# Attention over kept tokens: a step planner that places work by half steps, with row operands made earlier, norms tied to the scores of their step, and an early token load split in two

## The chip, the cores and the metric

The kernel runs on one core of one Trainium2 chip. The time is the device time of one execution in microseconds (us), the median over runs. Matrix products run on TensorE (PE in the profile, its weight loads PEld), sums and element-wise work on VectorE (DVE), exponentials and most copies out of PSUM on ScalarE (ACT), gathers and scatters of rows by index are issued from GpSimd (POOL), and all other transfers from SyncE (SP).

## The reference

```python
# x: (16, 512, 1024), mask: (16, 1024) of 0 and 1, 8 heads of 64
xt = transpose(x, (0, 2, 1))
q = xt @ Wq.T                                   # queries, keys and values are the same
scores = (1/8) * einsum('bhqd,bhkd->bhqk', qh, qh)
logits = (scores * cmask + (1 - cmask) * -1e30) * rmask
attn = softmax(logits)
ctx = einsum('bhqk,bhkd->bhqd', attn, qh)
out = x + transpose(ctx @ Wo.T, (0, 2, 1))
```

A masked key has no weight, and a masked query row sees all logits equal, so that its result is the mean of all values. About half of the 1024 tokens of a batch are kept.

## The kernel before

For each of the 16 batches, `slots` and `index` compute from the mask where each kept token goes (room for C = 544: four chunks of 128 and a tail of 32), and `gather` fetches the rows of the kept tokens in five transfers (L313). `xt` transposes the five chunks on PE (L398) and splits them into two float16 parts (high on ACT, L358; low on DVE, L359). `query(e, g)` makes a 128-row block e of q over half g of the tokens in 12 float16 matmuls (L421); ACT copies it out of PSUM (L424). `qsplit` splits q again (DVE), and SP spreads the parts over partitions (tiles `xx`, L442 to L445). `value(e)` transposes q back (L467), `value_tail` does so for the 32 tail tokens (L484, read out by DVE in L487). `top` (PE L509, DVE L511) and `bottom` (PE L518) turn row sums of squares into a bound for the exponent (`nm`).

`scores` makes 128 rows of scores of one head in four float16 matmuls (L580; the tails of four heads in L555) into one of two PSUM buffers of the tile `pss`, and ACT takes the exponential with its row sum (L584). So the third block of scores waits for the exponential of the first. `attend` multiplies two heads' weights with the values (eight float32 passes, `pav`, L598), and a fifth part covers the tail (L601). `recip_sums` and `recip_rows` make the reciprocals of the sums: DVE work, a PE transpose (L634), a copy `rr` (L637), a write to DRAM `rd`, and a broadcast read `rb`. `norm` multiplies `c` by `rb` (L665), fills the masked rows with the mean and splits the result into `ch` and `cl`. `project(i)` is 12 matmuls of 512 columns (L681), an addition to the token rows (`plus`, L686), and a scatter (L765). `project_tail` does the tails of up to three batches at once, and `rest` adds a mean row to the masked tokens (L752) and scatters them. `sum_half` (L343, ACT) sums token rows loaded in L337 and L348.

All PE results other than `pss` and `pav` share two PSUM buffers of the tile `pm`: the third user waits until the first has been read out.

The order is planned by hand in `run`. While batch b goes through 18 steps (two heads, 128 rows each; two steps are for tails), the list `m` holds other work with a PE cost in us beside each entry: tokens, queries and values of batch b+1, projections of batch b-1, the index of batch b+2. Each step first does what `free` holds for it, then both scores, then takes entries of `m` up to its even share, then two attends:

```python
ps = [self.scores(b, 2 * p, i)]
if i == 2 and whole:
    whole.pop()()
ps.append(self.scores(b, 2 * p + 1, i))
...
goal = total * (st + 1) / N
while pos < len(m) and (done + m[pos][0] / 2 <= goal or st == N - 1):
```

`late`, `gather` and `scatter` go to two lists, from which one transfer leaves per step; each waits for the latest matmul of scores or queries (`beat`). The additions of `rest` wait for `beat` as well. A scheduler behind the language may still move single instructions against the written order.

Of the kernel before, what the change touches and what calls it, by code (L numbers as in the profile page):

```python
# [49 lines left out]
class Fast:  # L50
# [114 lines left out]

    def slots(self, b0, b1):
# [7 lines left out]
        mb = self.sb([P, B, TB], F32, "sc", 3)  # L174
        nc.vector.tensor_scalar(mb, self.mt[:, bs], 0.5, None, ALU.is_gt)
        mh = self.sb([P, B, TB], F16, "tmp", 2)
        nc.vector.tensor_copy(mh, mb)
# [19 lines left out]
        ge = self.sb([P, NC, NB - 1], F16, "c", 3)  # L197
# [5 lines left out]
        oh = self.sb([P, NC, NB], F16, "c", 3)  # L203
# [6 lines left out]
    def facts(self, b0, b1):  # L210

# [17 lines left out]
        eh = self.sb([P, B], F16, "tmp", 2)  # L229
        nc.vector.tensor_copy(eh, e)  # L230
        pe = self.pm([P, B])
        nc.tensor.matmul(pe, lhsT=self.on16, rhs=eh, start=True, stop=True)
# [3 lines left out]

    def index(self, b):
        nc = self.nc
        s = self.st[b]
        ol = self.sb([P, TB, P], F16, "tmp", 2)  # L240
        lo = self.lo[:, b]
        nc.vector.tensor_tensor(ol, self.io128.unsqueeze(1).broadcast_to([P, TB, P]),
                                lo.unsqueeze(2).broadcast_to([P, TB, P]), ALU.is_equal)
# [185 lines left out]
    def qsplit(self, b, e):  # L429


        nc, s = self.nc, self.st[b]
        q = s["q"][:, e, :C]
        hl = self.sb([P, 3, C], F16, "hl", 2)
        nc.vector.tensor_copy(hl[:, 0, :], q)
        nc.vector.tensor_tensor(hl[:, 1, :], q, hl[:, 0, :], ALU.subtract)
        nc.vector.tensor_copy(hl[:, 2, :], hl[:, 0, :])
        xx = self.sb([P, 4, C], F16, "xx", 5)

        def spread():  # L440
            lo, up = slice(0, DK), slice(DK, P)
            nc.sync.dma_start(out=xx[lo, 0:2, :], in_=hl[lo, 0:2, :])  # L442
            nc.sync.dma_start(out=xx[up, 0:2, :], in_=hl[lo, 1:3, :])
            nc.sync.dma_start(out=xx[lo, 2:4, :], in_=hl[up, 0:2, :])
            nc.sync.dma_start(out=xx[up, 2:4, :], in_=hl[up, 1:3, :])  # L445

        self.later(spread)
        s["xx"].append(xx)
# [23 lines left out]

    def value_tail(self, b, g):
# [6 lines left out]
        q = self.sb([P, 2, HG, CT], F32, "qt")  # L480
        nc.scalar.copy(q, s["q"][:, 2 * g:2 * g + 2, 512:C].unsqueeze(2).broadcast_to([P, 2, HG, CT]))
# [13 lines left out]
    def shift(self, b, g):  # L495
        self.top(b, g)
        self.bottom(b, g)

    def top(self, b, g):

        nc, s = self.nc, self.st[b]
        hs = slice(HG * g, HG * g + HG)
        wide = self.smcol[g]
        sm = wide[:, :HG]
        nc.vector.tensor_reduce(sm.rearrange("p (e h) -> p e h", h=2),
                                s["sd"][:, 2 * g:2 * g + 2, :].rearrange("p e (k h) -> p e h k", h=2), AX.X, ALU.max)
        nc.vector.tensor_tensor(sm, sm, s["sdt"][:, hs], ALU.max)
        pt = self.pm([P, P])
        nc.tensor.transpose(pt, wide, self.ident)  # L509
# [32 lines left out]
    def scores(self, b, p, i):  # L542
# [6 lines left out]
        if i is None:  # L549
# [12 lines left out]
            hi = self.sb([P, C], F32R, "c", 3)  # L562
# [26 lines left out]
    def attend(self, b, p, i, ps):  # L589
# [13 lines left out]
        if i == 4:  # L603
            c = self.sb([P, C], F32, "c", 3)
# [41 lines left out]
    def norm(self, b, p):  # L646
# [18 lines left out]
        nc.vector.tensor_tensor(c, c, s["rb"][p], ALU.mult)  # L665
# [109 lines left out]
    def last(self, b, todo):  # L775
# [8 lines left out]
        self.recip(b, 3)  # L784
# [5 lines left out]
        for i in range(4):  # L790
            self.product(s["ch"], s["cl"], slice(i * P, (i + 1) * P), pos[i], range(3))
        self.norm(b, 3)
# [4 lines left out]
    def run(self, flag):  # L797
# [32 lines left out]
        for c in range(DC):  # L830
            self.load("q", c, 0)
        self.slots(0, 2)
        self.warm(36)
        self.index(0)
# [16 lines left out]
        def index1():  # L851
            with self.behind(self.last_xs):
                self.index(1)

        g1 = [(0, L(self.gather, 1, j)) for j in range(5)]

# [7 lines left out]
        first += [(0, lambda k=k: self.load_half(1, k, self.last_xt)) for k in range(DC)]  # L864
        first += value(0, 1) + [(0, L(self.value_tail, 0, 0))] + query(0, 2, 0) + g1[2:3] + query(0, 2, 1)[:1] + g1[3:4]
# [16 lines left out]
        begin = g1[4:] + [(1.5, lambda: None)] + query(0, 3, 0) + value(0, 2) + query(0, 3, 1) + value(0, 3)  # L882
        begin += [(0.3, L(self.value_tail, 0, 1)), (0, L(self.means, 0))]
# [4 lines left out]
        for b in range(B + 1):  # L888
            o, n = b - 1, b + 1
            if b == B:  # L890
                self.last(o, todo)
                break
            free, early, late = {}, ([], []), []
            if b >= 1:
                early = [(0, L(self.recip_sums, o, 3))], [(0.1, L(self.recip_rows, o, 3))]
                late = [(0, L(self.norm, o, 3))]
            if n < B:
                if b in tails:
                    free[0] = [L(self.late, o, 4)]
                    late += [(2.6, L(self.project_tail, o))]  # L900
                for x in rests.get(b, []):
                    free.setdefault(0, []).extend(L(self.late, x, j) for j in range(5, 9))
                    late += [(0, L(self.rest, x, j)) for j in range(5, 9)]
            chunk2 = [(0, L(self.norm, o, 2))] if b else []
            P_ = (lambda *i: project(o, *i)) if b else (lambda *i: [])
            tp, bt = [(0.1, L(self.top, b, 1))], [(0.1, L(self.bottom, b, 1))]
            if n < B:
                m = xt(n)[:1] + early[0] + xt(n)[1:2] + chunk2 + xt(n)[2:3] + early[1] + xt(n)[3:] + tp + query(n, 0, 0) + query(n, 0, 1) + bt + value(n, 0)
                m += query(n, 1, 0) + late + P_(0) + query(n, 1, 1) + P_(1)
                m += [(0, L(self.range_x, n, c)) for c in range(DC)]  # L910
                r = P_(2) + value(n, 1) + [(0.25, L(self.value_tail, n, 0))] + query(n, 2, 0) + query(n, 2, 1)
                r += query(n, 3, 0) + [(0.1, L(self.top, n, 0))] + value(n, 2) + query(n, 3, 1)
                r += [(0.1, L(self.bottom, n, 0))] + P_(3) + value(n, 3)
                r += [(0.25, L(self.value_tail, n, 1)), (0, L(self.means, n))]
                if b + 2 < B:
                    m += [(0.5, L(self.index, b + 2))]
                    r[1:1] = [(0, L(self.gather, b + 2, j)) for j in range(5)]
                if b == 0:
                    for c in range(DC):
                        r.insert(1 + 3 * c, (0, L(self.split, "o", c)))  # L920
                m += r
            else:

                places = [("xi", 8), ("xa", 13)]
                come = [[L(self.late, x, j, *places[k % 2]) for j in range(5, 9)] for k, x in enumerate(rests[b])]
                leave = [[L(self.rest, x, j) for j in range(5, 9)] for x in rests[b]]
                free[0] = [L(self.late, b, 4)] + come[0]
                for c, l in zip(come[1:] + [[]], leave):
                    free[0] += c + l
                m = chunk2 + early[0] + early[1] + tp + bt + [(2.6, L(self.project_means, b))] + late + P_(0, 1, 2, 3)  # L930
            for g in groups:
                if b == g[0] - 1:
                    m.insert(7, (0.1, L(self.facts, *g)))
                if b == g[0] - 2:
                    m.insert(7 if b == 0 else 0, (0.1, L(self.slots, *g)))
            if b == 1:
                m += [(0, L(self.range_w, "o", c)) for c in range(DC)]
            if b == B - 1:
                m.append((0.1, self.ranges))
            if b == 0:  # L940
                m = begin + m
            if b + 2 < B:
                self.start(b + 2)
                for c in range(DC):
                    at = 3 * c + (0 if b else 4)
                    free.setdefault(at, []).append(L(self.load_all, b + 2, c, None if b else first_top))
                    free.setdefault(at + 4, []).append(L(self.sum_half, b + 2, c))
            if b == 0:
                for k in range(3, 2 * DC):
                    if k >= DC:  # L950
                        free.setdefault(0, []).append(lambda k=k: self.load_half(1, k, first_top))
                    free.setdefault(k // 3, []).append(L(self.sum_half, 1, k))
            total = sum(c for c, _ in m)
            done, pos = 0.0, 0
            for st, (p, i) in enumerate(S):
                soon, self.soon = self.soon, []
                for f in soon + free.get(st, []):
                    f()
                if i is None:
                    self.scores(b, p, None)  # L960
                else:
# [181 lines left out]
```

## Time and profile before

| what | value |
|---|---|
| median of three runs | 1109.42 us (1104.3 to 1111.29) |
| profiled execution | 1102.9 us, of which span 1100.9 us |
| granted TensorE clock, mean | 0.997 |
| PE matmuls | busy 1066.3 us, 97% of the span |
| PE weight loads | 695.1 us |
| DVE | 735.7 us, 67% |
| ACT | 675.8 us, 61% |
| POOL | 295.2 us |

The busy time of PE counts each matmul from its start to its modelled end. Neighbours overlap, so a busy PE can still make pauses. The timeline gives the start of each matmul, and the distance from one start to the next tells the pace.

### The profile page before, as it was taken

How to read it: one execution, taken by the hardware profiler on the slowest of the kernel's cores; microseconds unless marked ns; L12 is line 12 of the kernel's file. 1: busy time of each engine (PE TensorE's matmuls, PEld its weight loads, DVE VectorE, ACT ScalarE, POOL GpSimd, SP SyncE). 2: the span in 40 equal slices, each digit the busy share in tenths (PEclk: the TensorE clock that was granted, in tenths of full speed). 3: DMA queues.
4: the chain of work that ended last, by engine and by line, in shares of the span. 5: the costliest groups of instructions: out<-in, count | busy, mean ns of one | idle time of the engine just before them, and what ended most of it. 6: DMA issues, size and time to landing. Idle time of an engine off the chain costs nothing.

```text
span 1100.9 us, 23215 instructions
## 1 busy us (share of the span) xinstructions
PE 1066.3 (97%) x8386; PEld 695.1 (63%) x8386; DVE 735.7 (67%) x2375; ACT 675.8 (61%) x1716; POOL 295.2 (27%) x303
## 2 busy tenths in 40 slices
PE   6899999999999999999999999999999999999997
PEld 6576666666666666666666666666666666666553
DVE  6797467765765757767674766856667675757653
ACT  5786566666666756657665666666656666655550
POOL 3101031323202222222322223232222322223652
PEclk9999999999999999999999999999999999999999
DMA  6755455646546464665655666455664655555752
GB/s 206 213 159 158 128 166 150 191 132 183 153 130 179 125 196 142 183 185 157 184 142 176 175 183 178 138 175 151 204 176 138 185 147 161 150 156 160 222 163 89
DMA packets 78121, 181.34 MB, mean 165 GB/s; under 512 B 15008, under 2 KB 16800, under 8 KB 78000
## 3 DMA queue, kind: packets, MB, share of 16 engines
q1 hardware_dynamic: 56816, 111.62, 36.3%
q0 software_dynamic: 21184, 68.18, 19.2%
q8 instruction: 68, 1.11, 0.4%
q14 instruction: 53, 0.43, 0.1%
HBM read 92.34 MB, written 33.91 MB: 115 GB/s over the span
## 4 chain that ended last, share of the span: by engine, by line
PE 72%; DVE 14%; DMA 6%; issue 4%; ACT 3%; SPq 1%; POOL 0%; DVEq 0%; POOLq 0%; ACTq 0%
PE pav L598 20%; PE pss L580 17%; PE pm L681 15%; PE pm L421 8%; PE pm L398 3%; PE pav L601 2%; DMA rb<-rd 2%; PE pm L467 2%; DVE c L665 2%; PE pm L634 1%; DMA rd<-rr 1%; ACT p L584 1%; PE pss L555 1%; DVE top L366 1%; DVE tmp L458 1%
## 5 line engine op out<-in xcount | busy, mean ns | idle before, releaser
L584 ACT ACTIVATE p<-pss,nm 128x544 f32<-128x544 f32 x512 | 363.2, 714 | 215.2 <-PE pss L580 208.0
L580 PE MATMUL pss<-xx 128*128 128x272 f16 x2048 | 301.6, 280 | 0.1
L598 PE MATMUL pav<-p,v 128*64 128x272 f32 x2048 | 278.8, 402 | 0.9 <-ACT c L605 0.9
L580 PEld LDWEIGHTS <-xx 128*128 128x128 f16 x2048 | 192.1, 99 | 77.9 <-issue 33.7
L598 PEld LDWEIGHTS pav<-p,v 128*64 128x64 f32 x2048 | 130.3, 136 | 98.4 <-issue 40.1
L421 PE MATMUL pm<-xh,wqh 128*128 128x274 f16 (+1 forms) x512 | 143.4, 280 | 0.1
L765 POOL DMA_INDIRECT y_out<-xa,idx x68 | 69.4, 1021 | 275.2 <-PE pss L580 169.5
L421 PE MATMUL pm<-xl,wqh 128*128 128x274 f16 (+1 forms) x512 | 142.9, 279 | 0.2 <-DVE xl L359 0.2
L421 PE MATMUL pm<-xh,wql 128*128 128x274 f16 (+1 forms) x512 | 143.1, 279 | 0.0
L313 POOL DMA_INDIRECT xa<-x_in,idx x68 | 68.7, 1010 | 183.8 <-PE pss L580 89.4
L421 PEld LDWEIGHTS <-wqh 128*128 128x128 f16 x1024 | 99.4, 99 | 23.1 <-issue 5.1
L584 ACT ACTIVATION_READ_ACCUMULATOR p<-pss,nm 128x1 f32 x512 | 102.8, 201 | 0.0
L313 POOL DMA_INDIRECT xi<-x_in,idx x60 | 61.8, 1030 | 142.7 <-PE pss L555 50.8
L686 DVE SCALAR_TENSOR_TENSOR xa<-pm,xa 128x512 f32<-128x512 f32 x60 | 41.4, 689 | 80.6 <-PE pm L681 80.4
L765 POOL DMA_INDIRECT y_out<-xi,idx x60 | 67.1, 1119 | 99.1 <-PE pss L580 51.0
L424 ACT ACTIVATE q<-pm 128x272 f32<-128x272 f32 (+1 forms) x128 | 51.1, 399 | 65.6 <-PE pm L421 65.1
L681 PE MATMUL pm<-woh,cl 128*128 128x512 f16 x240 | 91.0, 379 | 0.0
L681 PE MATMUL pm<-wol,ch 128*128 128x512 f16 x240 | 90.9, 379 | 0.0
L681 PE MATMUL pm<-woh,ch 128*128 128x512 f16 x240 | 90.9, 379 | 0.0
L665 DVE TENSOR_TENSOR c<-c,rb 128x544 f32<-128x544 f32 x64 | 46.3, 723 | 49.1 <-DMA rb<-rd 42.3
L681 PEld LDWEIGHTS <-ch 128*128 128x128 f16 x480 | 46.1, 98 | 40.4
L343 ACT ACTIVATE xm<-xm 128x1024 f32<-128x1024 f32 (+1 forms) x60 | 61.9, 1032 | 2.3 <-DMA xm<-x_nat_in 2.3
(191 smaller groups left out, 1560.8 us busy)
## 6 DMA issues: line engine op xcount, KB each, us to landing
xx<-hl SPq DMA_DIRECT2D x256, 136.0 KB
xm<-x_nat_in SPq DMA_DIRECT2D x56, 512.0 KB
rb<-rd SPq DMA_DIRECT2D x128, 136.0 KB
pt<-c SPq DMA_DIRECT2D x64, 136.0 KB
pt<-p SPq DMA_DIRECT2D x64, 136.0 KB
ub<-ud SPq DMA_DIRECT2D x16, 256.0 KB
xi<-x_nat_in SPq DMA_DIRECT2D x8, 256.0 KB
xa<-x_in,idx POOLq DMA_INDIRECT x68, 4.3
```

The costliest lines, as they stand in the source:

```text
L313: dma = self.nc.gpsimd.indirect_dma_start(out=tile[:n], out_offset=None, in_=self.x, in_offset=bass.IndirectOffsetOnAxis(ap=idx, axis=0))
L343: self.nc.scalar.activation(s["xm"][k], s["xm"][k], AF.Copy, accum_out=s["ms2"][:, k:k + 1])
L398: self.pe = nc.tensor.transpose(pt[:, c, :], x[:n, c * P:(c + 1) * P], self.ident[:n, :n]).ins
L421: self.beat = nc.tensor.matmul(pq, lhsT=w[:, c, e * P:(e + 1) * P], rhs=xx[:, c, cols], start=(k == 0), stop=(k == 3 * DC - 1)).ins
L424: nc.scalar.activation(s["q"][:, e, cols], pq, AF.Copy, scale=1.0 / (SX * SW))
L580: self.beat = nc.tensor.matmul(pt[:, g, :CH], lhsT=xx[:, 2 * k, i * P:(i + 1) * P], rhs=xx[:, 2 * k + a, g * CH:(g + 1) * CH], start=(a == ...
L584: self.exp = [nc.scalar.activation(t.rearrange("p (g c) -> p g c", g=2), pt[:, :, :CH], AF.Exp, bias=s["nm"][p // HG][:, p % HG:p % HG + 1 ...
L598: nc.tensor.matmul(s["pav"][k * DK:(k + 1) * DK, g, :CH], lhsT=s["v"][p][:, i, k * DK:(k + 1) * DK], rhs=ps[k][:, cols], start=(i == 1), s ...
L665: nc.vector.tensor_tensor(c, c, s["rb"][p], ALU.mult)
L681: nc.tensor.matmul(po[:cols.stop - cols.start], lhsT=a[:, e, cols], rhs=w[:, e, :], start=(e == 0 and k == 0), stop=(e == DC - 1 and k == 2))
L686: self.nc.vector.scalar_tensor_tensor(x, po, 1.0 / (SX * SW), x, ALU.mult, ALU.add)
L765: dma = self.nc.gpsimd.indirect_dma_start(out=self.out, out_offset=bass.IndirectOffsetOnAxis(ap=idx, axis=0), in_=x, in_offset=None)
```

## The change

The planner takes entries of `m` at two places of a step, between the two scores and after the attends, by a share for each (`share`). Some functions are cut in two, so that the DVE or ACT part stands earlier in the order than the matmul which uses it: `active` out of `slots`, `facts_sums` out of `facts`, `hot` out of `index`, `tail_copy` out of `value_tail`, `peaks` out of `top`. The order of `m` is new. `norm` of the first three head pairs waits for `beat`, and the first two come two steps later; the tile `c` has four buffers in place of three. Of batch 1, the second four loads of tokens come right behind the first spread of `xx` instead of after the first bound, all eight sums are placed in the steps of batch 0 (three of them are done twice: 75 sums in place of 72), and its first two `xt` come while batch 0 is being set up. In `last`, the reciprocal rows are transposed after a first part of a projection. The computation is the same: the number of matmuls does not change. The core of the diff:

```diff
-        ol = self.sb([P, TB, P], F16, "tmp", 2)
+    def hot(self, b):
+        ol = self.st[b]["ol"] = self.sb([P, TB, P], F16, "tmp", 2)
...
+    def tail_copy(self, b, g):
+        q = s["qt"] = self.sb([P, 2, HG, CT], F32, "qt")
+        self.nc.scalar.copy(q, s["q"][:, 2 * g:2 * g + 2, 512:C].unsqueeze(2).broadcast_to([P, 2, HG, CT]))
...
+    def peaks(self, b, g):
+        sm = self.smcol[g][:, :HG]
...
         nc.vector.tensor_tensor(sm, sm, s["sdt"][:, hs], ALU.max)
+    def top(self, b, g):
+        pt = self.pm([P, P])
+        nc.tensor.transpose(pt, self.smcol[g], self.ident)
...
-            hi = self.sb([P, C], F32R, "c", 3)
+            hi = self.sb([P, C], F32R, "c", 4)
...
-        nc.vector.tensor_tensor(c, c, s["rb"][p], ALU.mult)
+        self.once(nc.vector.tensor_tensor(c, c, s["rb"][p], ALU.mult), self.beat if p < 3 else None)
...
-        self.recip(b, 3)
+        self.recip_sums(b, 3)
...
             self.product(s["ch"], s["cl"], slice(i * P, (i + 1) * P), pos[i], range(3))
+            if i == 0:
+                self.recip_rows(b, 3)
...
+        def rest1():
+            with self.behind(self.last_xx):
+                for k in range(DC, 2 * DC):
+                    self.load_half(1, k)
...
-                m = xt(n)[:1] + early[0] + xt(n)[1:2] + chunk2 + xt(n)[2:3] + early[1] + xt(n)[3:] + tp + query(n, 0, 0) + query(n, 0, 1) + bt + value(n, 0)
-                m += query(n, 1, 0) + late + P_(0) + query(n, 1, 1) + P_(1)
-                r = P_(2) + value(n, 1) + [(0.25, L(self.value_tail, n, 0))] + query(n, 2, 0) + query(n, 2, 1)
-                r += query(n, 3, 0) + [(0.1, L(self.top, n, 0))] + value(n, 2) + query(n, 3, 1)
-                r += [(0.1, L(self.bottom, n, 0))] + P_(3) + value(n, 3)
-                r += [(0.25, L(self.value_tail, n, 1)), (0, L(self.means, n))]
-                    m += [(0.5, L(self.index, b + 2))]
-                    r[1:1] = [(0, L(self.gather, b + 2, j)) for j in range(5)]
+                    m = sums + pk(b, 1) + x[:2] + second + x[2:4] + rows + x[4:]
+                    m += q(0, 0) + tp(b, 1) + q(0, 1)
+                    m += bt(b, 1) + q(1, 0) + v(0) + third + q(1, 1)
+                    m += tc(0) + rng[:2] + tail + v(1) + P_(0) + tv(0) + rest + P_(1) + hot + rng[2:] + q(2, 0) + index
+                    m += pk(n, 0) + q(2, 1) + tp(n, 0) + P_(2) + take + v(2) + q(3, 0) + bt(n, 0)
+                    m += q(3, 1) + tc(1) + [(0, L(self.means, n))] + P_(3) + v(3) + tv(1)
...
+                share = [(1.2, 0) if i is None else ((0.95, 0.95), (0.9, 0), (0.45, 0.95), (0.9, 0))[i] for _, i in S]
+                unit = sum(c for c, _ in m) / sum(map(sum, share))
...
                         ps = [self.scores(b, 2 * p, i)]
                         if i == 2 and whole:
                             whole.pop()()
+                    fill(share[st][0], st == N - 1)
+                    if i is not None:
+                        ps.append(self.scores(b, 2 * p + 1, i))
...
-                            free.setdefault(st + 5, []).append(L(self.norm, b, p))
+                                free.setdefault(min(st + 7, N - 1), []).append(L(self.norm, b, p))
```

## The prediction

> **What bounds the kernel now.** First the page: span, busy times and clock.
>
> ```profile
> span 1100.9 us, 23215 instructions
> ...
> PE 1066.3 (97%) x8386; PEld 695.1 (63%) x8386; DVE 735.7 (67%) x2375; ACT 675.8 (61%) x1716; POOL 295.2 (27%) x303
> ...
> PEclk9999999999999999999999999999999999999999
> ```
>
> PE is the bound, and its clock is granted throughout, so time can only come out of its pauses. The 97% hides them, because overlapping matmuls are counted to their modelled ends. So, second, the timeline of PE, where the distance between starts is the pace.
>
> ```profile
> 345.46 1.09 PE L580 MATMUL pss<-xx 128*128 128x272 f16 x8
> 346.39 0.27 PE L509 MATMUL pm<-ident,smcol 128*128 128x128 f32 x1
> 346.50 0.60 PE L467 MATMUL pm<-ident,q 128*128 128x128 f32 x4
> 347.77 0.33 PE L634 MATMUL pm<-ident,rcol 128*128 128x128 f32 x1 [0.67 <-DVE m L511]
> 347.94 1.09 PE L580 MATMUL pss<-xx 128*128 128x272 f16 x8
> ```
>
> Eight score matmuls take 0.93 us to the next start, 0.116 each; a transpose takes 0.11. The four of L467 should be over at 346.94, yet L634 starts at 347.77: a pause of 0.83, of which the row's busy account shows 0.67. It waits for PSUM: the third user of `pm` needs the buffer of `top` (L509), which DVE's L511 reads late.
>
> Measured so, one pace per form: scores 2048 x 0.116 = 237.6 us; queries 1536 x 0.116 = 178.2; projections 852 x 0.216 = 184.0; attends 2048 x 0.124 (16 in 1.98 in the chain) = 253.5; their tails 256 x 0.125 = 32.0; tail scores 512 x 0.029 = 14.8; float32 transposes 672 x 0.109 = 73.2; the rest 17. Sum 990. From the first matmul (3.5) to the last (1093.3) are 1090 us, so **about 99 us are pauses**: 18 before 66 us, 77 from 66 to 1056, 3 to 4 behind. Of the 77, about 39 are what each change of kind takes everywhere (0.09 from float16 into an attend, 0.15 from `bottom`, 0.03 between attends), and **38 are waits**. By the matmul that waits: L634 11.5, scores 8.4, `xt` 7.5, `value` 5.0, others 6.
>
> Third, who ends PE's waits (total, times, longest), and the same for DVE.
>
> ```profile
> PE pm L634 <- DVE m L511: 5.5, 8, 0.9
> ...
> PE pss L398 <- DMA xa<-x_in,idx: 3.4, 1, 3.4
> PE pm L398 <- DVE tmp L487: 3.1, 3, 1.3
> PE pss L555 <- DMA xx<-hl: 2.7, 1, 2.7
> PE pm L634 <- DVE rcol L628: 2.4, 4, 0.8
> ```
>
> ```profile
> DVE c L665 <- DMA rb<-rd: 42.3, 27, 4.7
> ...
> DVE xi L752 <- PE pss L580: 17.2, 20, 1.9
> ```
>
> Many short waits for PSUM to be read out, two long ones in the head. DVE's 42.3 us on `rb` are no cost by themselves.
>
> **The change part by part.** For each wait I count, in the instruction order of both programs, the PE work that stands between cause and consumer (cover), priced by the pace.
>
> *1. Reciprocal rows, L634.* Before, 14 times the buffer of `top` is needed again after at most 0.93 us of work (0.44 in nine). After, one or two such places remain. The wait for the sums themselves (L628, L625: 3.0 of the 11.5) stays, since the work from the last scores to the transpose keeps its shortest 3 to 4 us. 11.5 - 3.0 = 8.5 saved; ends 0 and 11.5.
>
> *2. Scores between half steps.* The third block waits for an exponential of 0.714 + 0.201 = 0.915 us. Before, 124 of 517 blocks have under 1.5 us of other PE work for it, after 46 of 518. 8.4 x 46/124 = 3.1 stay: 5.3 saved; ends 0 and 7.
>
> *3. Transposes.* `xt` behind `xt` had ten covers of 0.2 to 1.2 us, and behind `value_tail` ten of 1.48 for L487; after, the smallest are 1.86 and 2.14. 7.5 falls to 2.5: 5.0 saved; ends 2 and 7.5. `value` waits for q: 27 of 58 begin with under 1.2 us between, after 10 of 57; 5.0 x 10/27 = 1.9 stays: 3.1 saved; ends 0 and 5.
>
> *4. New reuse of PSUM.* Ten queries and five L634 come 0.49 us behind the query whose buffer they need. Before, 18 values stood 0.46 to 0.49 behind a query and paused 0.05 to 0.19: 15 x 0.16 = 2.4. Fourteen `value_tail` come 0.9 us behind the projection whose buffer they need: L681's 0.38 + L686's 0.69 + two hand-overs of 0.04 = 1.15 from start to start, against 0.9 + 0.216 = 1.12. Free, DVE costs 0.03 each, behind one more operation of 0.69 it costs 0.72. I take 0.15, nearer the free end because L686 waits for PE 45 times (80.4 us) before: 2.1; ends 0.4 and 10. Five queries behind a projection: 0.5. Together +5.0.
>
> *5. Norms that wait for scores.* 48 multiplications now wait for a matmul. Behind them on DVE stand `xl`, `rr`, the sums and the read-outs that PE needs. No row shows this wait; the nearest is L752, which has it 64 times, idles DVE 17.2 + 2.6 us, and held PE's weight load once, for 0.4 us. 48/64 x 0.4 = 0.3, taken as 0. It replaces the wait for `rb`, two steps later, which also held that queue (a gain already in 1 to 3). Ends: 0, and 48 x 0.6 = 29 if PE always waited most of one norm operation (0.72).
>
> *6. Gathers later.* They stand behind the third projection. From the matmul that a gather waits for to its first transpose were at least 9.0 us of PE work, now in five batches 3.9 for the tail and 5.2 for the fourth chunk, elsewhere 7.7 or more. The trace lands these transfers 2.9 / 4.0 / 5.9 us (least, median, most) after issue. Five places at 0.4: 2.0; ends 0 and 5 x 2.0 = 10. [...]
>
> *7. Head.* SP issues the second four loads of batch 1 (256 KB each) from about 28.9 us, behind the first spread, instead of two at 32.8 and two at 39.7. At the 202 GB/s of the first 66 us, 1 MB takes 5.2 us and is over at 34.1, just as the next spread is issued (34.4), on which PE waited 2.7. One load of `wo` (256 KB) then stands ahead of it in place of two of tokens: 1 us saved; ends -2 (it collides) and 2.7. [...] The three sums done twice are 3 x (0.63 + 0.20) = 2.5 us of ACT, which is 45 of 66 us busy there: 0, end 2.5. The gather's 3.4 stays, as its chain is unchanged.
>
> *8. End.* `rr` to the last norm is one chain (1079.9 to 1085.8, then 2.3 us of DVE) beside 36 x 0.216 = 7.8 us of projections. Nine matmuls (1.9 us) now come first, and 0.3 to 0.8 us of pause ahead of L634 goes: +0.7; ends 0 and 1.9.
>
> *9. Changes of kind.* float16 to float32 and back: 678 before, 784 after. Priced by kind of neighbours the sum stays within 2 us (more attends behind scores, fewer behind queries and projections): 0; ends -4 and 53 x 0.17 = 9. Splitting functions adds no instruction but the three sums. `c` with four buffers covers the later norms. The first two `xt` of batch 1 move behind gathers issued well before: 0.
>
> Sum: -8.5 - 5.3 - 5.0 - 3.1 + 5.0 + 2.0 - 1.0 + 0.7 = -15.2. The profiled execution took 1102.9 (span 1100.9, 2.0 around it), so it becomes 1087.7. The median of the three runs, 1109.42, lies 6.5 higher; on its scale I predict **1094 us**, 1.4% less.
>
> **The rivals.**
> *A, all waits go* (chance 0.13). Better cover also takes the 6 us of others, nothing new appears: -38 - 2.7 + 3 = -38, hence 1072. For it: covers of scores, `value` and `top` all grow. Against: the fifteen covers of 0.49.
> *B, the pauses only move* (0.21). `value_tail` waits the full 10 for PSUM in place of 2.1, and gathers cost 10 in place of 2: -15 + 8 + 8 = 1, or 1110; half of it gives 1102. For it: 3.9 against a landing of up to 5.9.
> *C, slower by DVE* (0.16). Norms bound to PE's place hold back what PE needs next. From 15.2/48 = 0.32 us per norm the gain is gone; at 0.6 it is 1094 + 29 = 1123. For it: DVE is 67% busy, and `xl`, `rr` and read-outs with short cover stand behind. Against: L752's 0.4 us in all.
> *D, half steps that aren't* would be part of B: the scheduler may join what was written apart. In the order after, 71 score blocks still follow a score block directly, against 169, so most is real.
>
> **How the numbers follow.** The sum's case has 0.50; its own range, from the ends of terms 4, 6 and 7, is 1085 to 1103, and 0.08 of it lies within 1% of before (1098.3 to 1120.5). About 1% is what a measurement of this kernel can tell from no change. Faster by over 1%: 0.42 + 0.13 = 0.55; within: 0.08 + 0.21 = 0.29; slower: 0.16. The range 1074 to 1117 reaches A and the lighter half of C, and leaves out about 0.18.
>
> **What would show it.** L634 behind L511 gone from PE's waits; L584's wait for scores longer and scores' wait for L584 shorter; DVE L665 waiting for scores instead of `rb`; L487's wait gone; small pauses at queries (0.2) and `value_tail`; `xt` waiting for a gather in every third batch at most. The prediction is wrong if DVE's `xl`, `rr` or L686 become frequent releasers of PE (C), or if the pauses stay near 99 us (B).

## The result, and the profile after

| | before, same chip | after |
|---|---|---|
| median of four runs | 1109.97 us (1104.3 to 1111.29) | 1082.4 us (1079.31 to 1083.16) |
| profiled execution / its span | 1102.9 / 1100.9 us | 1082.2 / 1080.5 us |
| granted clock, mean | 0.997 | 0.993 |

The ratio, taken over all runs and not from the two medians, is 0.9762, with a 95% interval of 0.9739 to 0.9786: 2.4% faster, 1.7 times the forecast 1.4%. The forecast of 1094 us is 11.6 us too high.

The page of the kernel after:

```profile
span 1080.5 us, 23254 instructions
...
PE 1053.5 (98%) x8386; PEld 698.3 (65%) x8386; DVE 739.3 (68%) x2375; ACT 679.0 (63%) x1722; POOL 317.5 (29%) x303
...
PEclk8999999999999999999999999999999999999999
```

PE does the same 8386 matmuls in 20.4 us less, DVE and ACT are busy 3 to 4 us longer. So pauses went. One thing is worse: the clock of the first slice (8 tenths, 9 before). What ends PE's waits after (total, times, longest):

```profile
PE pm L186 <- DVE mh L173: 3.5, 1, 3.5
PE pss L611 <- ACT p L615: 2.3, 2, 1.7
PE pm L443 <- DVE xa L717: 2.2, 5, 1.1
...
PE pm L489 <- DVE q L449: 1.5, 4, 0.4
PE pss L586 <- DMA xx<-hl: 1.4, 1, 1.4
```

The lines have moved: scores are L611 (before L580), their exponential L615 (L584), the queries L443 (L421), the projections L712 (L681), `plus` L717 (L686), the transpose of reciprocals L665 (L634), the multiplication by `rb` L696 (L665). The transpose of reciprocals no longer waits for the read-out of `top`; it had 5.5 us in eight waits before. And DVE's waits after:

```profile
DVE xa L717 <- PE pm L712: 83.6, 52, 3.8
DVE xi L783 <- PE pss L611: 28.5, 19, 2.5
...
DVE c L696 <- SPq L1164: 5.0, 1, 5.0
```

The 42.3 us on `rb` are gone from the list. `plus` now waits for PE 52 times, so DVE is early where it was late.

Counted as in the prediction, one pace per form, the pauses of PE fell from 98.6 to 79.4 us: in the middle from 77.4 to 57.1, at the end from 3.4 to 1.9. In the head they rose from 17.7 to 20.3. The count is good to about 2 us: from the start of the first matmul to the start of the last are 1089.6 us before and 1068.4 after, so with the same matmuls at the same pace the pauses must have fallen by 21.2 us, where the count finds 19.2.

### The profile page after: what moved, and what is told of

Same layout as the page of the kernel before. It is cut to its first block, busy times and chain, and to the rows that moved or that the text cites. A ratio compares the mean times of both kernels' runs of the same rounds, so it can differ in the third digit from the quotient of the medians.

```text
span 1080.5 us, 23254 instructions
## 1 busy us (share of the span) xinstructions
PE 1053.5 (98%) x8386; PEld 698.3 (65%) x8386; DVE 739.3 (68%) x2375; ACT 679.0 (63%) x1722; POOL 317.5 (29%) x303
## 4 chain that ended last, share of the span: by engine, by line
PE 88%; DVE 5%; ACT 3%; issue 2%; DMA 1%; POOL 0%; another core or an unknown queue 0%; POOLq 0%; SPq 0%; ACTq 0%; DVEq 0%
PE pav L629 23%; PE pss L611 21%; PE pm L443 15%; PE pm L712 14%; PE pm L420 3%; PE pav L632 3%; PE pm L489 2%; PE pss L586 2%; PE pm L665 1%; ACT p L615 1%; PE pm L511 1%; ACT xm L365 1%; PE warm L303 1%; ACT p L590 1%; DVE p L596 1%
## 5 line engine op out<-in xcount | busy, mean ns | idle before, releaser
L615 ACT ACTIVATE p<-pss,nm 128x544 f32<-128x544 f32 x512 | 365.9, 717 | 231.8 <-PE pss L611 221.8
L611 PE MATMUL pss<-xx 128*128 128x272 f16 x2048 | 314.1, 280 | 3.2 <-ACT p L615 2.3
L629 PE MATMUL pav<-p,v 128*64 128x272 f32 x2048 | 273.5, 401 | 0.0
L611 PEld LDWEIGHTS <-xx 128*128 128x128 f16 x2048 | 193.1, 100 | 77.8 <-issue 31.3
L443 PE MATMUL pm<-xh,wqh 128*128 128x274 f16 (+1 forms) x512 | 143.7, 281 | 3.1 <-DVE xa L717 2.2
L443 PE MATMUL pm<-xh,wql 128*128 128x274 f16 (+1 forms) x512 | 143.2, 280 | 0.0
L443 PE MATMUL pm<-xl,wqh 128*128 128x274 f16 (+1 forms) x512 | 143.1, 280 | 0.0
L335 POOL DMA_INDIRECT xa<-x_in,idx x68 | 76.4, 1124 | 174.6 <-PE pss L611 64.4
L443 PEld LDWEIGHTS <-wqh 128*128 128x128 f16 x1024 | 99.1, 99 | 26.0 <-issue 7.1
L796 POOL DMA_INDIRECT y_out<-xi,idx x60 | 76.8, 1280 | 121.9 <-PE pss L611 43.3
L615 ACT ACTIVATION_READ_ACCUMULATOR p<-pss,nm 128x1 f32 x512 | 103.5, 202 | 0.0
L717 DVE SCALAR_TENSOR_TENSOR xa<-pm,xa 128x512 f32<-128x512 f32 x60 | 41.4, 690 | 87.7 <-PE pm L712 83.6
L335 POOL DMA_INDIRECT xi<-x_in,idx x60 | 62.1, 1036 | 109.8 <-PE pss L611 39.0
L712 PE MATMUL pm<-woh,ch 128*128 128x512 f16 x240 | 91.1, 379 | 0.0
L712 PE MATMUL pm<-woh,cl 128*128 128x512 f16 x240 | 91.0, 379 | 0.0
L712 PE MATMUL pm<-wol,ch 128*128 128x512 f16 x240 | 91.0, 379 | 0.0
L712 PEld LDWEIGHTS <-ch 128*128 128x128 f16 x480 | 46.4, 98 | 45.7 <-issue 1.3
L783 DVE TENSOR_TENSOR xi<-xi,ub 128x512 f32<-128x512 f32 (+1 forms) x60 | 41.3, 691 | 30.5 <-PE pss L611 28.5
```

What stands on the lines that cost most here:

```text
L335: dma = self.nc.gpsimd.indirect_dma_start(out=tile[:n], out_offset=None, in_=self.x, in_offset=bass.IndirectOffsetOnAxis(ap=idx, axis=0))
L443: self.beat = nc.tensor.matmul(pq, lhsT=w[:, c, e * P:(e + 1) * P], rhs=xx[:, c, cols], start=(k == 0), stop=(k == 3 * DC - 1)).ins
L611: self.beat = nc.tensor.matmul(pt[:, g, :CH], lhsT=xx[:, 2 * k, i * P:(i + 1) * P], rhs=xx[:, 2 * k + a, g * CH:(g + 1) * CH], start=(a == ...
L615: self.exp = [nc.scalar.activation(t.rearrange("p (g c) -> p g c", g=2), pt[:, :, :CH], AF.Exp, bias=s["nm"][p // HG][:, p % HG:p % HG + 1 ...
L629: nc.tensor.matmul(s["pav"][k * DK:(k + 1) * DK, g, :CH], lhsT=s["v"][p][:, i, k * DK:(k + 1) * DK], rhs=ps[k][:, cols], start=(i == 1), s ...
L712: nc.tensor.matmul(po[:cols.stop - cols.start], lhsT=a[:, e, cols], rhs=w[:, e, :], start=(e == 0 and k == 0), stop=(e == DC - 1 and k == 2))
```

## The experiments

Letters name the explanations. H: taking other work between the two scores brings the gain. O: the new order of `m` does. N: the norms bound to scores (below also: tied) do. P, formed after the first runs: the order and the bound norms bring it together, neither alone. Kernels e1, e2, e3 and e6 ran on one chip (before's median 1103.3 us), e4, e5, e7 and e8 on a second (1102.41), e9 to e12 on a third (1108.73). Ratios are to before on the same chip. e3, e9, e11 and e12 have line numbers of their own.

### e1: both scores, then the work

```diff
-                    fill(share[st][0], st == N - 1)
                     if i is not None:
                         ps.append(self.scores(b, 2 * p + 1, i))
+                    fill(share[st][0], st == N - 1)
```

> The changed kernel (1082.4 us) with both scores of a step placed before the other work, as before; all else of the change stays. Theory O (the new order of the other work brings the gain, by ending the waits for PSUM at the reciprocal rows and the token transposes and by putting attends behind scores): score blocks with under 1.5 us of cover rise from 46 to 65 only, so 1082 to 1087. Theory H (the half steps bring the gain): at least half of the 27 us is lost, 1096 or more.

Measured: 1076.84 us (1076.22 to 1077.94), ratio 0.9762 [0.9741, 0.9783], that of after to the fourth digit. H has fallen: with the new order, half steps bring nothing.

### e2: norms as before

```diff
-        self.once(nc.vector.tensor_tensor(c, c, s["rb"][p], ALU.mult), self.beat if p < 3 else None)
+        nc.vector.tensor_tensor(c, c, s["rb"][p], ALU.mult)
...
-                                free.setdefault(min(st + 7, N - 1), []).append(L(self.norm, b, p))
+                                free.setdefault(st + 5, []).append(L(self.norm, b, p))
```

> The changed kernel with the norms two steps earlier again and without their wait for scores. Theory O: PE's order hardly changes, so 1081 to 1087. Theory N (DVE, freed from waiting on the broadcast rows, brings the gain): the 42 us of idle DVE on these rows come back and with them half of the gain, 1093 or more.

Measured: 1115.43 us (1109.67 to 1123.88), ratio 1.0096 [1.006, 1.0133]. That is theory N's side, and more than it said: the whole gain is lost, and the kernel is slower than before. On this one chip e1 and e2 lie 38.6 us apart. PE's waits in e2:

```profile
PE pm L511 <- DVE xa L717: 24.8, 14, 3.9
PE pm L443 <- DVE xa L717: 6.8, 5, 2.1
```

and DVE's:

```profile
DVE c L696 <- DMA rb<-rd: 96.1, 41, 7.2
```

PE waits for `plus` to empty its PSUM buffer, and DVE, which should do it, waits for broadcast rows. The timeline of e2 shows one such place (start, duration, then in brackets the idle time before and what ended it):

```profile
151.97 1.11 SPq L673 DMA_DIRECT2D rb<-rd  x2
...
154.57 0.38 PE L712 MATMUL pm<-woh,cl 128*128 128x512 f16 x1
...
157.59 0.72 DVE L696 TENSOR_TENSOR c<-c,rb 128x544 f32<-128x544 f32 x1 [6.93 <-DMA rb<-rd]
158.35 0.39 DVE L697 SCALAR_TENSOR_TENSOR c<-nh,mq,c 128x160 f32<-128x160 f32 x1
158.65 0.68 DVE L717 SCALAR_TENSOR_TENSOR xa<-pm,xa 128x512 f32<-128x512 f32 x1
...
159.39 0.69 PE L511 MATMUL pm<-ident,qt 128*128 128x128 f32 x2 [3.54 <-DVE xa L717]
```

The multiplication of the norm stood at the head of DVE's queue 1.3 us before the read of `rb` was even issued. The projection's last matmul starts at 154.57, and `plus` could have run from 155 on; it stands behind the norm and comes at 158.65. The transpose of the tail (L511) needs that buffer and idles PE for 3.54 us. In the kernel after, DVE's timeline at the same place has a norm well ahead of the read-out and the next one well behind it:

```profile
151.14 0.72 DVE L696 TENSOR_TENSOR c<-c,rb 128x544 f32<-128x544 f32 x1
...
157.50 0.69 DVE L717 SCALAR_TENSOR_TENSOR xa<-pm,xa 128x512 f32<-128x512 f32 x1 [2.44 <-PE pm L712]
...
161.97 0.72 DVE L696 TENSOR_TENSOR c<-c,rb 128x544 f32<-128x544 f32 x1
```

Here `plus` waits for PE, not PE for `plus`, and the norm of the rows requested at 154.68 comes at 161.97.

### e3: operands with their users

```diff
+        self.tail_copy(b, g)
         q = s["qt"]
...
+        self.peaks(b, g)
         pt = self.pm([P, P])
         nc.tensor.transpose(pt, self.smcol[g], self.ident)
...
-                        m += [(0, L(self.facts_sums, *g))]
...
-                        m += [(0.1, L(self.facts_end, *g))]
+                        m += [(0.1, L(self.facts, *g))]
```

`hot` and `active` go back in the same way.

> The changed kernel with the parts that were cut off (peaks, copy of the tails, one-hot rows, active mask, sums of the facts) put back at the matmul that uses them. Theory O: 1082 to 1086, as the covers of PE's matmuls are the same as in the changed kernel (46 score blocks under 1.5 us, 73 uses of PSUM under 1 us). Theory E (earlier operands bring the gain): 1092 or more.

Measured: 1076.69 us (1074.9 to 1079.23), ratio 0.977 [0.9744, 0.9796]. Earlier operands have no part that this comparison could tell.

### e6: before, with half steps only

```diff
                     ps = [self.scores(b, 2 * p, i)]
                     if i == 2 and whole:
                         whole.pop()()
+                fill(share[st][0], st == N - 1)
+                if i is not None:
                     ps.append(self.scores(b, 2 * p + 1, i))
...
+                fill(share[st][1])
```

Like the change itself, the edit also drops an old rule that put the attends now before, now behind the other work of a step: they come between the two fills.

> The kernel before (1110 us) with the other work in its old order, but placed at half steps with the new shares. Theory O: score blocks with under 1.5 us of cover fall from 124 to 46 (some 5 us less waiting), but uses of PSUM with under 1 us of cover rise from 55 to 101 (3 to 8 us more), so 1105 to 1113. Theory H: most of the gain, 1095 or less.

Measured: 1106.53 us (1101.37 to 1113.73), ratio 1.0024 [0.9999, 1.005]. Alone, half steps bring nothing. The two largest entries among PE's waits in e6 are

```profile
PE pm L421 <- DVE m L511: 8.0, 10, 1.4
PE pm L681 <- DVE xa L686: 6.4, 4, 2.5
```

### e5 and e4: before with norms bound to scores, without and with half steps

```diff
-            c = self.sb([P, C], F32, "c", 3)
+            c = self.sb([P, C], F32, "c", 4)
...
-        nc.vector.tensor_tensor(c, c, s["rb"][p], ALU.mult)
+        self.once(nc.vector.tensor_tensor(c, c, s["rb"][p], ALU.mult), self.beat if p < 3 else None)
...
-                            free.setdefault(st + 5, []).append(L(self.norm, b, p))
+                            free.setdefault(min(st + 7, N - 1), []).append(L(self.norm, b, p))
```

> The kernel before with only the norms changed: two steps later, waiting for scores, four buffers for c. Theory P (the tie keeps DVE's queue from standing at a norm whose broadcast rows are still under way; this pays where PE soon needs what stands behind): in 44 of 57 norms of the kernel before DVE reaches the norm within 7 us of PE work after the transposing of the reciprocals, here in 17. In the old order little that PE needs stands behind, so 0 to 8 us less: ratio to before 0.993 to 1.0. Theory N2 (the norms alone are the gain): 0.985 or less.

Measured for e5: 1101.85 us (1099.5 to 1102.49), ratio 0.9992 [0.9979, 1.0006]. DVE's wait for `rb` falls from 42.3 to 3.8 us, and the time stays: in the old order that wait was harmless. What PE waits for there has not gone, as its waits in e5 show:

```profile
PE pm L634 <- DVE m L511: 9.3, 13, 0.8
```

> The kernel before with the norms changed and half steps, but the old order of the other work. Theory P with the new order needed as well: 0.988 to 1.002. Theory that norms and half steps together are the gain: 0.98 or less.

Measured for e4, which has e6's edit too: 1090.03 us (1089.31 to 1090.55), ratio 0.9892 [0.9867, 0.9917]. N alone and H alone bring nothing in the old order, together 1.1%. PE's waits for DVE's read-out of `top` in e4:

```profile
PE pm L421 <- DVE m L511: 2.4, 8, 0.6
PE pm L634 <- DVE m L511: 2.2, 4, 0.6
```

Between e6 and e4 only the norms differ. With the norms of before, DVE's wait for `rb` (41.1 us in e6) stood ahead of what PE needed: 10.9 of the 23.5 us that PE waits for DVE behind 66 us in e6 come within twelve DVE instructions after a multiplication that waited for `rb`, among them the four waits for `plus` (L686); in e4 it is 1.0 of 6.9. So half steps, too, pay only with the tie. Why they bring something in the old order (e4 against e5) and nothing in the new one (e1) is not shown.

### e7 and e8: late but not tied, tied but not late

e7 is after with e2's first edit alone, e8 after with e2's second edit alone.

> The changed kernel with norms written two steps later, but without their wait for scores. The scheduler moves them up: DVE meets them 2.9 us (quarter) and 4.7 us (median) of PE work after the transposing, just as with norms as before. Theory P: as slow as that one, ratio 1.005 to 1.015. Theory that the two later steps are what counts: 0.976 to 0.982.

Measured for e7: 1117.7 us (1108.89 to 1120.97), ratio 1.0124 [1.0068, 1.0181], with 96.0 us of DVE's waits on `rb`. To write the norm two steps later does nothing here: the scheduler moves it up again, and in DVE's order 60 of the 64 multiplications stand at the very place that they have in e2. It is the wait for a matmul that keeps the norm back.

> The changed kernel with norms tied to scores, but two steps earlier. DVE meets them about 5 us of PE work after the transposing (least 3.9), where the rows take 6 to 8 us to come back. Theory P: waits of 1 to 3 us on DVE remain, but without the early extremes: ratio 0.98 to 1.0. Theory that the tie alone is enough: 0.975 to 0.98.

Measured for e8: 1088.73 us (1086.22 to 1092.39), ratio 0.9879 [0.9843, 0.9915]: the tie without the two steps leaves half of the gain. DVE still waits 29.8 us for `rb`, and PE 6.9 us for `plus` at the queries.

### e9 and e10: new order without the rest, tied and untied

e9 is after with e1's and e3's edits, so that of the change the order of `m` (with its shares ahead of and behind the attends), the tied late norms, the head and the end (`last`) remain. e10 is e1 with e2's edits.

> The changed kernel with both scores together and with the cut-off parts back at their users: what stays is the new order, the tied and later norms, and the loads in the head. If half steps and early operands each bring nothing and don't stand in for one another, the ratio is 0.974 to 0.979; if one stood in for the other, 0.983 or more.

Measured for e9: 1083.64 us (1082.09 to 1084.82), ratio 0.9767 [0.9744, 0.979]. The whole gain is there.

> The changed kernel with both scores together and norms as before (early, untied). In this order no tail transpose needs the PSUM of a projection within 1 us of cover (14 do in the changed kernel), so little stands behind DVE's waiting norms. Theory P: much milder than the 1.01 of the untied norms with half steps, 0.982 to 0.998. Theory that untied norms are slow in any new order: 1.005 or more.

Measured for e10: 1123.03 us (1121.87 to 1123.28), ratio 1.0123 [1.0096, 1.0149], 39.4 us above e9 on the same chip. P had expected a far smaller loss, because in e10 no tail transpose stands under 1 us behind the projection whose buffer it needs; the number went to its rival. PE's waits in e10:

```profile
PE pm L511 <- DVE xa L717: 16.2, 12, 4.7
PE pm L443 <- DVE xa L717: 4.1, 5, 1.3
```

DVE's longest wait for `rb` there is 6.7 us, so a cover of 1 us does not protect. P holds with this amendment: the new order needs the tie, with or without half steps. The ratios to before side by side (e2, e10 and after also have the earlier operands, which brought nothing in e3 and e9):

| | norms as before | norms tied and late |
|---|---|---|
| old order | 1 | 0.9992 (e5) |
| old order, half steps | 1.0024 (e6) | 0.9892 (e4) |
| new order | 1.0123 (e10) | 0.9767 (e9) |
| new order, half steps | 1.0096 (e2) | 0.9762 (after) |

Which part of the new order gains was not taken apart further.

### e11 and e12: the head

e11 is e9 with a head in which PE is kept busy:

```diff
-        self.warm(60)
+        self.warm(90)
...
+            if b == 0 and p == 0:
+                t = self.ps_av.tile([P, P], F32, tag="av", name="warm")
+                with self.behind(self.beat):
+                    for _ in range(24):
+                        self.nc.tensor.matmul(t, lhsT=self.on16, rhs=self.on16, start=True, stop=True)
```

> The new order with tied norms, both scores together, operands with users, and 54 more idle matmuls in the head: 30 before the first token rows land, 24 ahead of the first tail scores, where PE waits. The results of the idle matmuls are not used. If the half clock granted for 3.4 to 6.8 us near 14 and 40 us comes from these pauses, it goes: 2 to 5 us less than the same kernel without them, ratio 0.970 to 0.976; if not, or if they delay what they stand before, 0 to 3 us more.

Measured: 1080.89 us (1078.35 to 1083.23), ratio 0.9742 [0.9716, 0.9768]. This is 2.75 us under e9, with ranges that overlap. The ratio is the one expected if the half clock goes, but it did not go: it came at 14.6 us (for 6.8, as in e9) and again at 45.3 (for 3.4; in e9 at 41.9 for 6.8). So the cause of the 2.75 us is open.

e12 is e9 with the loads of batch 1 as before:

```diff
-        first += [(0, lambda k=k: self.load_half(1, k, self.last_xt)) for k in range(DC)] + [(0, rest1)]
+        first += [(0, lambda k=k: self.load_half(1, k, self.last_xt)) for k in range(DC)]
...
-                    for k in range(2 * DC):
-                        free.setdefault(1 + k // 3, []).append(L(self.sum_half, 1, k))
+                    for k in range(3, 2 * DC):
+                        if k >= DC:
+                            free.setdefault(0, []).append(lambda k=k: self.load_half(1, k, first_top))
+                        free.setdefault(k // 3, []).append(L(self.sum_half, 1, k))
```

> The new order with tied norms, both scores together, operands with users, and the second four loads of batch 1 as in the kernel before, behind the first bound (sums once). Prediction: the earlier loads save 1 us, so 0 to 2 us more than with them, ratio 0.974 to 0.981. Rival, that they collide with the spread: 1 to 3 us less.

Measured: 1078.81 us (1076.58 to 1081.28), ratio 0.9731 [0.9708, 0.9755], the best of all kernels: 4.8 us under e9 on the same chip, and the two ranges are apart. The stretch from 30 to 48 us, in e9 (length; busy time and instructions of PE, PEld, DVE, ACT, POOL; clock; DMA share; GB/s):

```profile
30.00:48.00 18.00, 12.22 (x86) 8.18 (x89) 8.97 (x27) 11.95 (x36) 3.25 (x4) 0.83 0.84 242
```

and in e12:

```profile
30.00:48.00 18.00, 15.31 (x127) 10.70 (x128) 13.52 (x42) 14.25 (x42) 2.87 (x3) 1.00 0.74 214
```

PE's longest wait for the spread of `xx` in e9:

```profile
PE pss L589 <- DMA xx<-hl: 4.3, 1, 4.3
```

In e12 it is

```profile
PE pss L589 <- DMA xx<-hl: 2.5, 1, 2.5
```

In e9, with the early loads, the DMA engines are busier (0.84 against 0.74), PE's wait for the spread ends later (at 44.20 us against 40.58), and half clock is granted for 6.8 us around the end of the wait (from 41.9 us). The first `attend` starts at 49.1 us in e9 and at 43.9 in e12. The sums moved together with the loads, so their share in the 4.8 us is not told apart. The length of the wait in one execution is a weak witness: it was 1.4 us in after's profile and 5.1 in e1's, and the first `attend` comes at 45.9 and 45.6. Steadier is the flight of the transfer of `xx` that PE waits for: from issue to landing it takes 4.0 to 4.6 us in the five kernels with the loads as before (before, e4, e5, e6, e12) and 4.4 to 7.6 in the nine with the early ones. That speaks for a collision, but the two ranges overlap, and it does not give a price.

## Why the prediction was right and where it was wrong

The call (faster by over 1%) and the place (pauses of PE that end in the reading out of PSUM) were right. The size was not. The call held because the change has the tie in it; the prediction gave the tie no part in the gain. Of the signs that it named, L634's wait behind L511 did go, but DVE's multiplication waiting for scores in place of `rb` hardly came (2.0 us in after). By the prediction's steps, in us of the profiled executions (waits and changes of kind are told apart by a price for each pair of neighbours, so a line is good to 1 to 2 us):

| step | predicted | measured |
|---|---|---|
| 1, L634 | -8.5 | 11.5 to 2.9: -8.6 |
| 2, scores | -5.3 | 8.2 to 6.2: -2.0 |
| 3, `xt` | -5.0 | 7.5 to 1.1: -6.4 |
| 3, `value` | -3.1 | 5.0 to 4.3: -0.7 |
| 4, new PSUM reuse | +5.0 | queries 1.5 to 7.0, `value_tail` 0.3 to 1.7: +6.9 |
| 5, norms | 0 | not told apart in a single trace, see below |
| 6, gathers | +2.0 | no wait for a gather in the middle: 0 |
| 7, head | -1.0 | 17.7 to 20.3: +2.6 |
| 8, end | +0.7 | 3.4 to 1.9: -1.5 |
| 9, changes of kind | 0 | 37.8 to 28.5: -9.3 |

With 2.0 us less in waits at attends these add up to -21.0; the profiled executions differ by 20.7 us. The medians differ by 27.6, since the profiled execution of before lay 7.1 us under its median and that of after 0.2 under: the forecast added 6.5 us to come to the scale of the medians. So of its 11.6 us too many, about 6 are that step and 5.5 the sum. That the sum is only 5.5 off is in part luck: some lines lie 11 us too low in all, others 17 too high.

**The step that was mis-sized: 9.** The sum "priced by kind of neighbours" was to stay "within 2 us". It fell by 9.3, although the number of changes rose from 678 to 784. The price of a change hardly moved: from scores to an `attend` the median pause is 0.092 us in both traces, from `bottom` to an `attend` 0.155, from an `attend` to `xt` 0.114. What moved is who stands beside whom. In the middle (66 to 1056 us before, 66 to 1036 after), changes from a query to an `attend` (2.7 us in total) went from 29 to 0, from a projection to an `attend` (2.2 us) from 24 to 0, from `bottom` to an `attend` (2.2 us) from 14 to 1, and from scores to an `attend` rose from 82 to 141 (9.0 to 13.0 us). With one price for each pair of neighbours in both traces (the lower quartile of its pauses) the sum falls from 40.0 to 33.9 us. So about 6 of the 9.3 are this new mix: the prediction named its direction ("more attends behind scores, fewer behind queries and projections") and put it at nothing. Of the rest, a part are short waits at changes that stayed, as from `xt` to scores: 25 and 29 of them, with 1.9 us before and 0.1 after.

**Steps 1 and 3 (`xt`)** held to within 1.4 us: the cover, counted in the instruction order, told what would go. For scores and `value` the waits went by less than in proportion to the counted covers, so that proportion is the part that failed; of the 6.2 us of scores after, 1.7 are a single wait at 1017 us. **Step 4** had the right sign and was 1.9 us short. Its smallest part, five queries behind a projection, put at 0.5 us, became 2.2 (L443 behind L717 above).

**Step 5 failed in its reasoning, not in its number.** It put the tie at no cost, and booked what it replaces as "a gain already in 1 to 3". The runs show no gain without the tie: new order and tie give -2.3% to -2.4% (after, e1, e3, e9), the new order without the tie +1.0% to +1.2% (e2, e7, e10), the tie alone 0 (e5). L634's waits for the read-out of `top` are gone from e2's list as well; longer waits, for `plus`, stand in their place. Reading before's 42.3 us of DVE on `rb` as harmless was right for before (e5 removes 38.5 of them for nothing). It was not carried over to the new order, where the same wait, without the tie, becomes 85 to 96 us and stands ahead of what PE needs.

**Rival C** named the right place, DVE's queue at the norms, with the sign the wrong way round: holding the norm back does not hold up the read-outs, it lets them pass. The threshold it gave, 0.32 us for each of 48 norms, was not reached in after, where PE's listed waits for DVE come to 4.2 us behind the one at the start, 0.09 per norm; without the tie PE waits 31.6 us for `plus` alone (e2), 0.66 per norm. **Rival D**, half steps that aren't: most were real, and they did not matter (e1). **Rivals A and B**: neither did all waits go, nor did pauses only move.

**Step 6** took the gather's landing time as a wait at five places. None came. **Step 7** had the wrong sign. It weighed a collision of the spread with the early loads and chose the gain; e12 against e9 shows the loss (4.8 us, loads and sums together), and the flights of `xx` speak for the collision. From 30 to 48 us e9 moved 242 GB/s with a wait of 4.3 us, e12 214 with 2.5. Loads and spread are both issued from SP, so the runs do not show where they meet. The end of -2 us that the step gave for a collision was the author's estimate, and no run shows it.

## What to carry to other kernels

Here a wait of DVE, which is not the bound, cost nothing in the old order (e5 removes 38.5 us of it, ratio 0.9992). In the new order something that PE needs stood behind it, and PE waited 31.6 us for `plus` (e2). So before work is reordered, look in each engine's queue for instructions that wait on a transfer (here 42.3 us on `rb`), and bind them to an event that comes after the transfer, not only to a later place in the text, which the scheduler undid here (in e7 60 of 64 multiplications stand where they do in e2). When parts of a change are undone one by one, undo them also in pairs and add them singly to the old kernel: here each of two parts was worth nothing or less alone.

## What the runs showed of the hardware

In e2 the granted clock was 0.50 around the end of four waits of PE in the middle of the kernel. At the 3.54 us shown above it is

```profile
158.70:165.50 6.80, 6.11 (x26) 3.11 (x27) 4.69 (x17) 1.46 (x4) 0.88 (x1) 0.50 0.04 11
```

There are two such places more, from 298.6 and 571.7 us, with waits of 3.95 and 3.68 us that end at 299.49 and 572.29, each 6.8 us long, and one of 3.4 us from 424.9, behind a wait of 2.09 that ends at 423.58. That is 23.8 us at half clock, or, by an estimate that takes PE as always at work in them, up to 12 us on top of the waits themselves. The page of e2 shows the three long ones as eights:

```profile
PEclk9999989999899999999989999999999999999999
```

The length of one wait does not tell whether half clock follows: in before, a wait of 3.43 us that ends at 15.07 us is followed by none (the clock from 12 to 24 us is 1.00), in e2 the one of 2.09 us is. What decides is not shown.

In the head, after spent 10.2 us at half clock (14.9 for 6.8, 42.2 for 3.4) where before spent 3.4 (from 40.6). The 6.8 us more can cost up to 3.4 by the same estimate, enough for the 2.6 us by which its head grew; that they are the cause is not shown.
